# Aggregating a four-head graph-attention layer transposed, in column groups of the array

## The chip, the cores and the metric

One core of a Trainium2 chip runs the whole program. The time is device microseconds from start to end of one execution; the kernel before takes 3029.77 us (median of three runs, 3027.55 to 3030.76). The profile is of one execution with a span of 3030.3 us.

## What is computed

A stack of four graph-attention layers on 32 batch items of 512 nodes with 256 features, all in fp32. Each layer is normalised first and added to its input. Layer 2, which the change touches, has four heads of 64 features:

```python
def _L2_gnn_ref(h, adj, W, a):
    N_H, D_F = (4, 64)
    Wh = (h @ W).reshape(h.shape[0], h.shape[1], N_H, D_F)
    ...
    e = s_src[:, :, None, :] + s_dst[:, None, :, :]
    e = jnp.where(e > 0, e, NEG_SLOPE * e)
    e = jnp.where(mask, e, -jnp.inf)
    alpha = jax.nn.softmax(e, axis=2)
    h_out = jnp.einsum('bijh,bjhd->bihd', alpha, Wh)
    ...
    return jax.nn.elu(h_out)
```

The kernel doesn't form the softmax with an exponential per edge. Since the exponential of a leaky ReLU of a sum is the larger of two products, a common factor of each row can be taken out. What remains for an edge from node j to node i is `p_j * max(r_i, t_j) * mask`. The factor `p_j` is put into the features of node j, so the weights of a head are one maximum and one product per edge, and the sum over j of the same weights with `p_j` alone is the softmax's denominator.

## The kernel before

The 512 nodes are four tiles of 128. Four streams (`NS = 4`) each take every fourth batch item through all the layers. A stream is a generator that yields a due time, worked out in `after_us` from the matmul columns issued so far and a given delay; the main loop always continues the stream that is due first. So the order in which the program is written is a mixture of four batch items in different layers, and each engine executes its part of the order that a scheduler makes of it. TensorE works through one queue for all streams: a matmul that waits holds up those of other streams behind it. Each stream has two banks of PSUM (`bank`, 128 x 512 fp32).

`matmul` (line 66) and `transpose` (line 70) are helpers, so the profile puts all matmuls on L68 and all transposes on L72. A matmul is called with the stationary operand second and the moving operand third: `matmul(p, w, x)` gives `w` transposed times `x`.

Layer 2 (`layer2`, line 424) runs so for each batch item:

- `turned` transposes the normalised input; for each node tile two matmuls with 268 columns (line 430) give, for all four heads, 64 features and three logits (`CH` = 67). ScalarE takes the exponentials of the logits (line 434: `p`, `t`, `r`), and VectorE multiplies the features with `p` (line 435). The tile `v` holds per node and head 64 features times `p`, then `p`, then `t`, `r`.
- `begin(h)` calls `weights` (line 335): four transposes spread `r` of the head along the free axis of a bank, and four VectorE instructions (line 343, 128 x 512 each) make the weights `w` of the head: partition = source node j, free = target node i, one instruction for each tile of j.
- The aggregation of a head (line 457): for each of four tiles of target nodes, four matmuls accumulate over j. The stationary operand is a 128 x 128 block of the weights, the moving operand the 65 columns `v[:, j, h, :D + 1]`: 64 features and `p`. The result has target nodes on partitions, and its 65th column is the denominator.
- One reciprocal (through `reciprocal`, line 359) and one product (line 461) divide; after every second head ScalarE and VectorE form the ELU of both heads and add it to `x` (lines 468 to 470).

The weights of head h + 1 are begun before the aggregation of head h.

Of the kernel before, what the change touches and what calls it, by code (L numbers as in the profile page):

```python
# [19 lines left out]
FP = mybir.dt.float32  # L20
# [3 lines left out]
AF = mybir.ActivationFunctionType  # L24
OP = mybir.AluOpType
# [3 lines left out]
P = 128  # L29
# [7 lines left out]
def fast(ctx, tc, flag, x, adj, w0, a0, w1, a1, w2, a2, mlp1_w, mlp1_b, mlp2_w, mlp2_b,  # L37
         w_fc, a_fc, w_hand, a_hand, out):
    nc = tc.nc
    B, N, F = x.shape  # L40
    NT = N // P
# [3 lines left out]
    NH = a2.shape[0]  # L45
    D = F // NH
# [5 lines left out]
    const = ctx.enter_context(tc.tile_pool(name="const", bufs=1))  # L52
    work = ctx.enter_context(tc.tile_pool(name="work", bufs=2))
# [5 lines left out]
    spent = [0.0]  # L59
    pace = [1.0] * NS  # L60

    def after_us(us):

        return begun[0] + pace[turn[0]] * (STRETCH * spent[0] / CYCLES + SLOW * us)

    def matmul(p, w, x, **flags):
        spent[0] += 4 * max(x.shape[-1], P)
        nc.tensor.matmul(p, w, x, **flags)  # L68

    def transpose(p, x, i):  # L70
        spent[0] += 2 * P
        nc.tensor.transpose(p, x, i)  # L72

    def bank():
        return psum.tile([P, N], FP, tag=f"b{turn[0]}", name="b", bufs=8 // NS)
# [3 lines left out]
    ident = const.tile([P, P], FP, name="ident")  # L79
# [3 lines left out]
    minus1 = const.tile([P, 1], FP, name="minus1")  # L83
    nc.vector.memset(minus1, -1.0)
    seen = const.tile([P, 5 * B], FP, name="seen")

    def load_x(b):
        t = work.tile([P, NT, F], FP, tag="x", name="x", bufs=NS + 1)
        nc.sync.dma_start(t, x[b].rearrange("(t p) f -> p t f", p=P))
        return t  # L90
# [16 lines left out]
    def project(dst, block, k, a_cols):  # L107

        ft, n = a_cols.shape[1], a_cols.shape[2]
        p = bank()  # L110
        for f in range(ft):
            transpose(p[:, f * P:(f + 1) * P], block(k, f), ident)
        wT = work.tile([P, N], FP, tag="y", name="wT", bufs=3)
        nc.scalar.copy(wT[:, :ft * P], p[:, :ft * P])
        q = bank()
        for f in range(ft):
            matmul(
                q[:, :n], wT[:, f * P:(f + 1) * P], a_cols[:, f, :], start=(f == 0), stop=(f == ft - 1)
            )
        nc.vector.tensor_copy(dst, q[:, :n] if len(dst.shape) == 2 else q[:, :n].rearrange("p (h c) -> p h c", c=3))  # L120
# [36 lines left out]
    for h in range(NH):  # L157
        t, r = divmod(h * D, P)
# [38 lines left out]
    for j in range(NT):  # L197
        turn[0] = j % NS
        p = bank()
# [49 lines left out]
    def small(shape, name):  # L249
        return work.tile([P] + shape, FP, tag=name, name=name, bufs=2 * NS)  # L250

    def new_xn():
        return work.tile([P, NT, F], FP, tag="xn", name="xn", bufs=3)

    def norm(xt, xn, rs, t0, late):


        st = small([2, 6], "st")
        mv = small([2, 2], "mv")
        for i in range(2):  # L260
            nc.vector.bn_stats(st[:, i, :], xt[:, t0 + i, :])  # L261
            nc.vector.bn_aggr(mv[:, i, :], st[:, i, :])
        rp = rs[:, t0:t0 + 2]
        nc.scalar.activation(rp, mv[:, :, 1], AF.Ln, bias=eps)
        nc.scalar.activation(rp, rp, AF.Exp, scale=-0.5)
        for i in range(2):
            if late:
                nc.vector.tensor_scalar(
                    xn[:, t0 + i, :], xt[:, t0 + i, :], mv[:, i, 0:1], 0.0, op0=OP.subtract, op1=OP.max
                )  # L270
            else:
                nc.vector.tensor_scalar(  # L272
                    xn[:, t0 + i, :], xt[:, t0 + i, :], mv[:, i, 0:1], rp[:, i:i + 1], op0=OP.subtract, op1=OP.mult
                )
# [9 lines left out]
    def turned(xn, when):  # L284

        hT = work.tile([P, KF, N], FP, tag="hT", name="hT", bufs=3)
        turn_pair(xn, hT, 0)
        yield when
        turn_pair(xn, hT, 2)
        yield after_us(0.6)  # L290
        return hT
# [3 lines left out]
    def note(e):  # L295

        c = next(noted)
        nc.vector.tensor_reduce(seen[:, c:c + 1], e, AX.XY, OP.max)  # L298
# [36 lines left out]
    def weights(r_col, t_col, masked=True):  # L335

        r = bank()
        for t in range(NT):
            transpose(r[:, t * P:(t + 1) * P], r_col(t).to_broadcast([P, P]), ident)
        wt = work.tile([P, NT, N], FP, tag="w", name="w", bufs=4)  # L340
        for j in range(NT):
            if masked:
                nc.vector.scalar_tensor_tensor(  # L343
                    wt[:, j, :], r, t_col(j), maskT[:, j, :], op0=OP.max, op1=OP.mult
                )
            else:
                nc.vector.tensor_scalar(wt[:, j, :], r, t_col(j), None, op0=OP.max)  # L347
        return wt

    def pair(tag="y"):  # L350
        return work.tile([P, 2, F], FP, tag=tag, name=tag, bufs=3)

    def aggregate(p, wt, t, rhs):
        for j in range(NT):
            matmul(p, wt[:, j, t * P:(t + 1) * P], rhs(j), start=(j == 0), stop=(j == NT - 1))

    def reciprocal(den):
        r = small([1], "rden") if len(den.shape) == 2 else small([NH, 1], "rden4")
        nc.vector.reciprocal(r, den)  # L359
        return r  # L360
# [14 lines left out]
    def add_elu(xr, r, q):  # L375

        nc.vector.scalar_tensor_tensor(r, q, 1.0, r, op0=OP.min, op1=OP.add)
        nc.vector.scalar_tensor_tensor(xr, r, -1.0, xr, op0=OP.add, op1=OP.add)
# [45 lines left out]
    def layer2(xt, xn, rs, when):  # L424
        hT = yield from turned(xn, when)
        v = work.tile([P, NT, NH, CH], FP, tag="v", name="v2", bufs=4)
        for t in range(NT):
            ps = bank()
            for k in range(KF):
                matmul(  # L430
                    ps[:, :NH * CH], hT[:, k, t * P:(t + 1) * P], W2[:, k, :, :], start=(k == 0), stop=(k == KF - 1)
                )
            pv = ps[:, :NH * CH].rearrange("p (h c) -> p h c", c=CH)
            nc.scalar.activation(v[:, t, :, D:], pv[:, :, D:], AF.Exp, scale=rs[:, t:t + 1])
            nc.vector.scalar_tensor_tensor(
                v[:, t, :, :D], pv[:, :, :D], rs[:, t:t + 1], v[:, t, :, D:D + 1].to_broadcast([P, NH, D]),
                op0=OP.mult, op1=OP.mult,
            )
            yield after_us(0 if t + 1 < NT else 1)
        ya = work.tile([P, NT, F], FP, tag="y4", name="y4", bufs=2)  # L440
        wts = []

        def begin(h):
            wts.append(weights(lambda t: v[:, t, h, D + 2:D + 3], lambda j: v[:, j, h, D + 1:D + 2]))
            return after_us(3.2)

        when = begin(0)
        note(v.rearrange("p t h c -> p (t h) c")[:, :, D:])
        yield after_us(1)
        for h in range(NH):  # L450
            last = when
            if h + 1 < NH:
                when = begin(h + 1)
            yield last
            wt = wts[h]
            p = bank()
            for t in range(NT):
                aggregate(p[:, t * (D + 1):(t + 1) * (D + 1)], wt, t, lambda j: v[:, j, h, :D + 1])
            pv = p[:, :NT * (D + 1)].rearrange("p (t c) -> p t c", c=D + 1)
            r = reciprocal(pv[:, :, D:])  # L460
            nc.vector.tensor_tensor(
                ya[:, :, h * D:(h + 1) * D], pv[:, :, :D], r.to_broadcast([P, NT, D]), op=OP.mult
            )
            if h % 2:
                c = slice((h - 1) * D, (h + 1) * D)
                y = ya[:, :, c]
                q = pair("q").rearrange("p a (b f) -> p (a b) f", f=2 * D)
                nc.scalar.activation(q, y, AF.Exp)
                nc.scalar.activation(y, y, AF.Relu)
                add_elu(xt[:, :, c], y, q)  # L470
            yield after_us(0)
        xn, rs = new_xn(), small([NT], "rs")
        for t0 in range(0, NT, 2):
            norm(xt, xn, rs, t0, False)
        yield after_us(7)
        return xn, rs, after_us(2)
# [241 lines left out]
    ready = {i: i * LEAD for i in range(NS)}  # L718
# [3 lines left out]
    while ready:  # L722
        i = min(ready, key=ready.get)
# [21 lines left out]
    p = bank()  # L745
# [401 lines left out]
@with_exitstack  # L1147
def kernel(ctx: ExitStack, tc: tile.TileContext, *args):
    nc = tc.nc
    keep = ctx.enter_context(tc.tile_pool(name="keep", bufs=1))  # L1150
    flag = keep.tile([1, 1], I32, name="flag")
    fast(tc, flag, *args)
    bad = nc.values_load(flag[0:1, 0:1], min_val=0, max_val=1)
    with tc.If(bad > 0):
        general(tc, *args)
# [27 lines left out]
```

## Time and profile before

| What | Value | From |
|---|---|---|
| Span of the profiled execution | 3030.3 us | page, first line |
| Mean granted TensorE clock | 0.990 | clocks of the cores |
| Records of TensorE matmuls, all lines | 15529 | page, part 1 |
| Aggregation of layer 2, 65 columns | 4096 records, mean 274 ns | groups with shapes kept apart |
| TensorE waiting for another engine's weights in all layers (weight loads on line 343) | 31.6 us, 73 times | waits |
| First projection to last aggregation of one batch item's layer 2 | 756.4 to 805.2 us | starts of 268- and 65-column records |
| First projection of the next stream's layer 2 | 848.6 us | the same |

The page names engines by short names: PE is TensorE's matmul, PEld its weight load, DVE is VectorE, ACT is ScalarE, POOL is GpSimd. A row of the groups gives the line, the engine, the operation, the tiles written and read, the shape, the count, then the busy time in us and the mean duration in ns of one record, and behind the second bar the idle time of the engine just before these instructions with what ended it. Records of TensorE overlap in the trace, since a matmul's end is modelled with the time it takes to leave the array; so the busy time of a group is the union of its records, and the mean is longer than the distance from one to the next. A row of the timeline merges neighbours of the same line and tiles: start, duration to the end of the last, and how many.

### The profile page before, as it was taken

To read this page: it belongs to the slowest core of one execution; us is meant where nothing else is said; L and a number is where in the kernel's file an instruction comes from. 1 tells how busy PE (TensorE), PEld (TensorE's weight loads), DVE (VectorE), ACT (ScalarE), POOL (GpSimd) and SP (SyncE) were. 2 spreads that over 40 slices of the span, in tenths; PEclk is the share of its full clock that TensorE was granted. 3 is DMA by queue.
4 is the path that set the end of the run, shared out by engine and by line. 5 is a ranking of instruction groups with operands and counts; after the bars stand their busy time and mean duration, and the time that the engine had idled before them with its cause. 6 is when DMAs were issued, how large, how long until landed. Compare 5 with 4: busy or idle time off the path is not lost. (4 is left out here: it accounts for less than half of the span.)

```text
span 3030.3 us, 43501 instructions
## 1 busy us (share of the span) xinstructions
PE 2924.8 (97%) x15529; PEld 2368.3 (78%) x15529; DVE 2269.9 (75%) x5674; ACT 1489.6 (49%) x3758; POOL 470.2 (16%) x509
## 2 busy tenths in 40 slices
PE   7999999999999999999999999999999999999897
PEld 5787887877788877788877788877888877788665
DVE  4588778777877777777778777877877877767664
ACT  3444455554455554455554455554455554454445
POOL 0011111101111201112111111101111111111111
PEclk8999999999999999999999999999999999999999
DMA  3022223222223222223232223222223222212220
GB/s 91 1 88 87 75 74 102 83 90 88 74 74 102 84 89 83 80 74 102 78 95 82 81 74 102 83 90 91 71 74 102 89 84 87 74 52 82 84 97 29
DMA packets 178685, 245.46 MB, mean 81 GB/s; under 512 B 15328, under 2 KB 153886, under 8 KB 178464
## 3 DMA queue, kind: packets, MB, share of 16 engines
q1 hardware_dynamic: 148704, 144.32, 14.9%
q0 software_dynamic: 29760, 98.30, 9.8%
q8 instruction: 125, 2.05, 0.3%
q14 instruction: 96, 0.79, 0.1%
HBM read 127.46 MB, written 115.12 MB: 80 GB/s over the span
## 5 line engine op out<-in xcount | busy, mean ns | idle before, releaser
L68 PE MATMUL b<-v,w 128*128 128x257 f32 (+1 forms) x7232 | 1225.5, 322 | 22.0 <-DVE w L343 8.6
L68 PEld LDWEIGHTS b<-v,w 128*128 128x128 f32 x7232 | 1054.2, 192 | 186.7 <-issue 51.7
L343 DVE SCALAR_TENSOR_TENSOR w<-b,v,maskT 128x512 f32<-128x512 f32 x896 | 635.7, 743 | 13.3 <-PE b L72 10.5
L68 PE MATMUL b<-WFC,oT 128*128 128x256 f32 (+1 forms) x2048 | 491.5, 380 | 0.8 <-ACT v L311 0.5
L68 PEld LDWEIGHTS b<-WFC,oT 128*128 128x128 f32 x2048 | 373.6, 189 | 50.8 <-issue 1.0
L68 PE MATMUL b<-W,hT 128*128 128x259 f32 (+1 forms) x1536 | 389.1, 391 | 9.8 <-DVE v L315 8.6
L68 PEld LDWEIGHTS b<-W,hT 128*128 128x128 f32 x1536 | 282.8, 192 | 60.2 <-DVE v L315 11.0
L571 POOL DMA_INDIRECT order<-v,at x248 | 251.1, 1013 | 462.7 <-DVE seen L298 139.9
L68 PE MATMUL b<-hT,WM 128*128 128x512 f32 x512 | 251.9, 598 | 8.2 <-ACT hT L282 7.8
L359 DVE RECIPROCAL rden<-b 128x1 f32<-128x1 f32 (+1 forms) x516 | 80.2, 163 | 233.6 <-PE b L68 230.6
L677 POOL TENSOR_TENSOR x<-x,y 128x512 f32<-128x512 f32 x64 | 81.2, 1269 | 1077.3 <-ACT y L675 980.8
L619 POOL DMA_INDIRECT g<-table,at x124 | 122.5, 988 | 790.8 <-ACT y L639 287.1
L68 PE MATMUL b<-oT,WM 128*128 128x512 f32 x512 | 232.8, 597 | 0.0
L261 DVE BATCH_NORM_STATS2 st<-x 128x6 f32<-128x256 f32 x512 | 193.2, 409 | 5.6 <-DMA x<-in_x_dram 2.7
L331 ACT ACTIVATE oT<-b,bias 128x512 f32<-128x512 f32 x128 | 87.5, 686 | 216.6 <-PE b L68 216.4
L384 DVE TENSOR_TENSOR y<-q,y 128x512 f32<-128x512 f32 x192 | 132.5, 691 | 67.1 <-ACT q L383 48.2
L72 PEld LDWEIGHTS b<-ident,xn 128*128 128x128 f32 x1024 | 125.9, 142 | 69.9 <-DVE xn L272 23.6
L493 ACT ACTIVATE v<-b,ends 128x256 f32<-128x256 f32 x256 | 120.3, 470 | 122.2 <-PE b L68 115.6
L72 PE MATMUL b<-ident,xn 128*128 128x128 f32 x1024 | 159.7, 278 | 20.4 <-DVE xn L272 8.7
L282 ACT ACTIVATE hT<-b 128x512 f32<-128x512 f32 x256 | 150.2, 593 | 40.7 <-PE b L72 39.6
L68 PEld LDWEIGHTS b<-oT,WM 128*128 128x128 f32 x512 | 95.3, 191 | 93.5 <-issue 91.4
L638 ACT ACTIVATE q<-g,rden 128x512 f32<-128x512 f32 x124 | 89.5, 722 | 145.9 <-DVE rden L359 142.7
(139 smaller groups left out, 3735.0 us busy)
## 6 DMA issues: line engine op xcount, KB each, us to landing
table<-sums SPq DMA_DIRECT2D x62, 1032.0 KB
sums<-order SPq DMA_DIRECT2D x62, 516.0 KB
x<-in_x_dram SPq DMA_DIRECT2D x32, 512.0 KB
out_dram<-x SPq DMA_DIRECT2D x64, 256.0 KB
sums<-order SPq DMA_DIRECT2D x62, 129.0 KB
order<-v,at POOLq DMA_INDIRECT x248, 2.5
g<-table,at POOLq DMA_INDIRECT x124, 4.5
adj<-in_adj_dram SPq DMA_DIRECT2D x1, 1024.0 KB
```

Source lines behind the costliest of these rows:

```text
L68: nc.tensor.matmul(p, w, x, **flags)
L72: nc.tensor.transpose(p, x, i)
L261: nc.vector.bn_stats(st[:, i, :], xt[:, t0 + i, :])
L282: nc.scalar.activation(hT[:, :, t0 * P:(t0 + 2) * P], p.rearrange("p (k n) -> p k n", k=KF), AF.Relu)
L331: nc.scalar.activation(o[:, f, :], p, AF.Relu, bias=bias[:, f:f + 1])
L343: nc.vector.scalar_tensor_tensor(wt[:, j, :], r, t_col(j), maskT[:, j, :], op0=OP.max, op1=OP.mult)
L384: nc.vector.tensor_tensor(r, q, r, op=OP.add)
L493: nc.scalar.activation(halves[c][:, t, :F], ps[:, :F], AF.Copy, scale=ends[:, t, 0:1])
L571: nc.gpsimd.indirect_dma_start(out=orders[c], out_offset=bass.IndirectOffsetOnAxis(ap=at[:, 0, t:t + 1], axis=0), in_=halves[c][:, t, :], ...
L619: nc.gpsimd.indirect_dma_start(out=g, out_offset=None, in_=table, in_offset=bass.IndirectOffsetOnAxis(ap=at[:, 1, t:t + 1], axis=0),)
L638: nc.scalar.activation(q, z, AF.Exp, scale=rd)
L677: nc.gpsimd.tensor_tensor(xr, xr, y, op=OP.add)
```

## The change

The aggregation of layer 2 is turned round. The features become the stationary operand (64 columns) and the weights the moving one (512 columns), so that the result has features on partitions and target nodes along the free axis. Two heads are done together: head `a` writes partitions 0 to 63 of a bank and head `a + 1` partitions 64 to 127, which puts their matmuls in two column groups of 64 columns of TensorE's array. Eight matmuls (four tiles of j, two heads) replace 32.

The denominators are no longer a 65th column. A tile `sums_of_p` holds for each node, tile and head 32 columns, of which the first is `p` and the others zero. For each pair of heads 16 matmuls with these 32 columns as stationary operand and 256 target nodes as moving operand use four column groups of 32: two heads times two halves of the target nodes.

Both results are copied to SBUF by ScalarE (`aT`, `dT`) and transposed back in six transposes per pair, after which the division and the ELU go on as before. Both runs of matmuls are in a block of high priority so that nothing of another stream comes between them, and the order over j and heads in the first is reversed so that its first matmul is the one whose weights come last. `begin` for the two heads of the next pair is now called between the runs of the present one. The helper `matmul` charges a half or a quarter of the columns in the planner's account (`beside`) for these matmuls. The output tile `y4` holds two heads instead of four and has one buffer instead of two.

```diff
-    def matmul(p, w, x, **flags):
-        spent[0] += 4 * max(x.shape[-1], P)
-        nc.tensor.matmul(p, w, x, **flags)
+    def matmul(p, w, x, beside=1, **flags):
+        spent[0] += 4 * max(x.shape[-1], P) / beside
+        return nc.tensor.matmul(p, w, x, **flags)
...
+    sums_of_p = const.tile([P, NT, NH, 32], FP, name="sums_of_p")
+    nc.vector.memset(sums_of_p, 0.0)
...
             nc.scalar.activation(v[:, t, :, D:], pv[:, :, D:], AF.Exp, scale=rs[:, t:t + 1])
+            nc.scalar.activation(sums_of_p[:, t, :, 0:1], pv[:, :, D:D + 1], AF.Exp, scale=rs[:, t:t + 1])
...
-        ya = work.tile([P, NT, F], FP, tag="y4", name="y4", bufs=2)
...
-        when = begin(0)
+        begin(0)
         note(v.rearrange("p t h c -> p (t h) c")[:, :, D:])
         yield after_us(1)
-        for h in range(NH):
-            last = when
-            if h + 1 < NH:
-                when = begin(h + 1)
-            yield last
-            wt = wts[h]
+        begin(1)
+        ready = after_us(6)
+        for a in range(0, NH, 2):
+            yield ready
+            aT = work.tile([P, N], FP, tag="aT", name="aT", bufs=1)
             p = bank()
-            for t in range(NT):
-                aggregate(p[:, t * (D + 1):(t + 1) * (D + 1)], wt, t, lambda j: v[:, j, h, :D + 1])
-            pv = p[:, :NT * (D + 1)].rearrange("p (t c) -> p t c", c=D + 1)
-            r = reciprocal(pv[:, :, D:])
-            nc.vector.tensor_tensor(
-                ya[:, :, h * D:(h + 1) * D], pv[:, :, :D], r.to_broadcast([P, NT, D]), op=OP.mult
-            )
...
+            with tc.high_priority():
+                for j in range(NT)[::-1]:
+                    for h in (1, 0):
+                        matmul(
+                            p[h * D:(h + 1) * D, :], v[:, j, a + h, :D], wts[a + h][:, j, :], beside=2,
+                            start=(j == NT - 1), stop=(j == 0),
+                        )
+            nc.scalar.copy(aT, p)
             yield after_us(0)
+            dT = work.tile([P, HN], FP, tag="dT", name="dT", bufs=1)
+            p = bank()
+            with tc.high_priority():
+                for j in range(NT):
+                    for i in range(2):
+                        for h in range(2):
+                            g = 32 * (2 * i + h)
+                            m = matmul(
+                                p[g:g + 32, :HN], sums_of_p[:, j, a + h, :], wts[a + h][:, j, i * HN:(i + 1) * HN],
+                                beside=4, start=(j == 0), stop=(j == NT - 1),
+                            )
+                            if j + g == 0:
+                                tc.keep_in_program_order(m)
+            nc.scalar.copy(dT, p[:, :HN])
+            when = after_us(0.8)
+            y = work.tile([P, NT, 2 * D], FP, tag="y4", name="y4", bufs=1)
+            for i in range(2):
+                if a + 2 < NH:
+                    yield after_us(0)
+                    begin(a + 2 + i)
+                    ready = after_us(5)
+                yield when
+                p = bank()
+                for c, part in enumerate((aT[:, i * P:], aT[:, (2 + i) * P:], dT[:, i * P:])):
+                    transpose(p[:, c * P:(c + 1) * P], part[:, :P], ident)
+                r = small([2, 2, 1], "rden4")
+                nc.vector.reciprocal(r, p[:, 2 * P:3 * P].rearrange("p (i h c) -> p i h c", i=2, h=2)[:, :, :, 0:1])
...
```

More of the change, by code (lines that the diff above doesn't have):

```diff
@@ L439, in layer2 @@
             yield after_us(0 if t + 1 < NT else 1)
-        ya = work.tile([P, NT, F], FP, tag="y4", name="y4", bufs=2)
+        HN = N // 2
         wts = []
@@ L444, in begin @@
             wts.append(weights(lambda t: v[:, t, h, D + 2:D + 3], lambda j: v[:, j, h, D + 1:D + 2]))
-            return after_us(3.2)
-        when = begin(0)
+        begin(0)
         note(v.rearrange("p t h c -> p (t h) c")[:, :, D:])
         yield after_us(1)
-        for h in range(NH):
-            last = when
-            if h + 1 < NH:
-                when = begin(h + 1)
-            yield last
-            wt = wts[h]
-            p = bank()
-            for t in range(NT):
-                aggregate(p[:, t * (D + 1):(t + 1) * (D + 1)], wt, t, lambda j: v[:, j, h, :D + 1])
-            pv = p[:, :NT * (D + 1)].rearrange("p (t c) -> p t c", c=D + 1)
-            r = reciprocal(pv[:, :, D:])
-            nc.vector.tensor_tensor(
-                ya[:, :, h * D:(h + 1) * D], pv[:, :, :D], r.to_broadcast([P, NT, D]), op=OP.mult
-            )
[L464 to L470, printed above, removed]
-            yield after_us(0)
@@ new lines, in layer2 @@
+        begin(1)
[3 more added lines that the diff above has]
+            aT = work.tile([P, N], FP, tag="aT", name="aT", bufs=1)
+            p = bank()
+            with tc.high_priority():
[6 more added lines that the diff above has]
+            nc.scalar.copy(aT, p)
+            yield after_us(0)
+            dT = work.tile([P, HN], FP, tag="dT", name="dT", bufs=1)
[25 more added lines that the diff above has]
+                nc.vector.reciprocal(r, p[:, 2 * P:3 * P].rearrange("p (i h c) -> p i h c", i=2, h=2)[:, :, :, 0:1])
+                nc.vector.tensor_tensor(
+                    y.rearrange("p (k i) (h d) -> p k i h d", k=2, h=2)[:, :, i, :, :],
+                    p[:, :2 * P].rearrange("p (k h d) -> p k h d", k=2, h=2), r.to_broadcast([P, 2, 2, D]), op=OP.mult
+                )
+                when = after_us(0)
+            c = slice(a * D, (a + 2) * D)
+            q = pair("q").rearrange("p a (b f) -> p (a b) f", f=2 * D)
+            nc.scalar.activation(q, y, AF.Exp)
+            nc.scalar.activation(y, y, AF.Relu)
+            add_elu(xt[:, :, c], y, q)
@@ L472, in layer2 @@
+        yield after_us(0)
         xn, rs = new_xn(), small([NT], "rs")
```

## Prediction

> **What bounds the kernel now.** I read the page's first two parts first: which engine is full, and whether it is full all the time.
>
> ```profile
> PE 2924.8 (97%) x15529; PEld 2368.3 (78%) x15529; DVE 2269.9 (75%) x5674; ACT 1489.6 (49%) x3758; POOL 470.2 (16%) x509
> ...
> PE   7999999999999999999999999999999999999897
> ...
> PEclk8999999999999999999999999999999999999999
> ```
>
> TensorE is busy 97% of the span in every slice but the ends, at full clock. VectorE follows at 75%. So a change is worth what it adds to or takes from TensorE's stream, as long as it makes TensorE wait no longer. Next, the groups of instructions with shapes kept apart, for what layer 2 puts into that stream:
>
> ```profile
> L68 PE MATMUL b<-v,w 128*128 128x65 f32 x4096 | 476.9, 274 | 5.7 <-DVE y L461 2.0 <-DVE seen L298 1.2 <-DVE at L566 1.2
> L68 PE MATMUL b<-WFC,oT 128*128 128x256 f32 x1024 | 245.9, 380 | 0.8 <-ACT v L311 0.5 <-ACT tj L545 0.3
> L68 PE MATMUL b<-oT,WM 128*128 128x512 f32 x512 | 232.8, 597 | 0.0
> L72 PE MATMUL b<-ident,v 128*128 128x128 f32 x896 | 132.5, 274 | 11.8 <-DVE v L315 11.8
> L343 DVE SCALAR_TENSOR_TENSOR w<-b,v,maskT 128x512 f32<-128x512 f32 x896 | 635.7, 743 | 13.3 <-PE b L72 10.5
> ```
>
> The program issues 32 batches x 4 heads x 16 = 2048 matmuls with 65 columns, and the trace has 4096 records: one fp32 matmul is two records. A transpose is one (896 = 224 x 4). The means (274 ns) contain a tail that overlaps the next record, so the price is the pitch, read from stretches of one shape in the timeline:
>
> ```profile
> 1499.74 0.83 PE L68 MATMUL b<-v,w 128*128 128x65 f32 x6
> 1500.41 2.81 PE L68 MATMUL b<-WFC,oT 128*128 128x256 f32 x12
> ...
> 1503.49 1.03 PE L68 MATMUL b<-WFC,oT 128*128 128x256 f32 x4
> 1504.35 0.60 PE L72 MATMUL b<-ident,v 128*128 128x128 f32 x4
> 1504.79 0.60 PE L68 MATMUL b<-v,w 128*128 128x257 f32 x2
> ...
> 1516.75 3.65 PE L68 MATMUL b<-oT,WM 128*128 128x512 f32 x8
> 1520.24 1.00 PE L68 MATMUL b<-v,w 128*128 128x65 f32 x8
> ```
>
> From the start of one row to the start of the next: six 65-column records take 0.67 us, **112 ns** each; four of 256 take 0.86 us, **215**; eight of 512 take 3.49 us, **436**; four transposes 0.44 us, **110**. A 65-column record costs half of a 256-column one for a quarter of the columns: that waste is what the change goes after. 4096 x 112 ns = 459 us, 15% of the span.
>
> **What the Trainium skill says.** (1) "TensorE: Matmul & The Clock Gate", section LDWEIGHTS: a weight load takes its columns divided by 1.2 GHz, whatever the moving operand. For 128 columns that is 107 ns; the 112 ns of a 65-column record agree. (2) "FP8 and Floating Point Precision", TensorE Precision Notes: true fp32 is four passes through the array. The trace shows two records per matmul, each some twice its columns long (215 ns for 256): four passes in two records, both of one instruction and so of one column group. (3) "TensorEngine Tiling (Array Packing)", Key Properties: tiles of the array run in parallel, and a change of tiling mode drains the engine. No matmul of the kernel before is tiled, so the trace is silent. (4) "TensorE: Matmul & The Clock Gate", Part 3, The mechanism: matmuls start and end in program order; only weight loads are pulled ahead. No record of before contradicts it, and none tests it with groups.
>
> **The change part by part** (per pair of heads; there are 32 x 2 = 64 pairs).
>
> Removed: 32 matmuls of 65 columns, 64 records x 112 ns = 7.17 us.
>
> Added, features: 8 matmuls with 64 stationary columns and 512 moving ones, 16 records of 436 ns. Heads alternate between two column groups. By (2) the two records of one matmul share a group, so they follow each other; by (4) the next matmul, in the other group, can't start before the second record of this one has. What overlaps is then the second record of one matmul with the first of the next: 8 matmuls take 9 slots, 9 x 436 = 3.92 us. Bounds: 8 x 436 = 3.49 if the groups are fully free of each other, 16 x 436 = 6.98 if groups don't overlap in fp32.
>
> Added, sums of p: 16 matmuls with 32 stationary columns and 256 moving ones in four groups, 32 records of 215 ns. **Here is the choice that decides.** If four groups ran freely, 8 x 215 = 1.72 us. By the same argument as above only neighbours overlap, two at a time, however many groups there are: 17 x 215 = 3.66 us. In series it would be 6.88. I take 3.66.
>
> Added, transposes: 6 x 110 ns = 0.66 us, in whole-array mode.
>
> Added, changes of mode: into and out of each of the two tiled runs, up to four per pair. A drain is bounded below by 0 and above by the tail of a record, 380 - 215 = 165 ns (256-column row). Half: 4 x 0.083 = 0.33 us. In the issue order of the changed kernel all 64 feature runs stand as 8 in a row and all 64 runs of sums as 16 in a row, so there are no more changes than that.
>
> Sum on TensorE: 3.92 + 3.66 + 0.66 + 0.33 = 8.57 against 7.17: +1.40 us a pair, x 64 = **+90 us**.
>
> Waits: a feature run starts only when the weights of both heads are there, 8 x 743 ns = 5.9 us of VectorE, and stands at the head of TensorE's queue with the other streams' matmuls behind it. In the new order some 6 to 9 us of TensorE work lie between the first head's transposes and its run, so the slack is 0 to 3 us where VectorE is prompt. Before, TensorE's weight loads waited for these weights 31.6 us in all. I take +5 us net, between -20 and +40.
>
> ScalarE: per batch four more small exponentials (172 to 272 ns, rows of lines 311 and 434) and copies of 512 and 256 columns (578 and 371 ns, rows of lines 545 and 604), two of each: about 2.8 us, x 32 = 90 us on an engine that is busy 1490 of 3030. At nothing: three other streams' matmuls stand between the copies and the transposes that need them. VectorE keeps four reciprocals and four 256-element products per batch (176 and 416 ns): nothing. The single buffers of sums_of_p, aT, dT and y4 are shared by the streams, but layer 2 of a batch lasts some 48 us (first projection 756.4, last aggregation 805.2), and the next stream's begins 92 us after it (848.6): nothing. The zeroing of sums_of_p lies in the load of the first data: nothing.
>
> **The rivals.**
> - *Two at a time* (forecast): 3029.8 + 90 + 5 = 3125, of which I take 3120, since some sum runs follow their feature run at once, which saves a change of mode. For it: two records per matmul, program order. It needs nothing beyond what the trace and the skill say.
> - *Groups run free*: 3.49 + 1.72 + 0.66 + 0.33 = 6.20 us, -0.97 a pair, -62 us, +5 of waits: about 2973. This is what the change counts on (it charges a half and a quarter for such matmuls), and the Part 3 of (4) reports 2.38 times for three column groups. Against it: no statement there has two records per matmul. With full drains and late weights it shrinks to 2995.
> - *No overlap in fp32*: 6.98 + 6.88 + 0.66 + 0.2 = 14.7 us, +7.5 a pair, +480 us: about 3510. The reported speed-up speaks against it.
> - *The weights arrive late*: with groups free but 1 us of waiting at each of 64 feature runs, -62 + 64: 3030, no change. VectorE at 75% speaks for some of it, the 31.6 us of before against so much.
>
> **How the numbers follow.** Two at a time 0.48, groups free 0.38, no overlap 0.07, late weights with free groups 0.07. The predicted time is that of the first. Its own spread, with 0 to 165 ns per drain and -20 to +40 us of waits, is 3090 to 3165; that of free groups 2945 to 3000. The range 2960 to 3155 holds both but their ends, and leaves out about 2 in 10 (no overlap, the deepest gain, the worst loss). Faster: 0.37 of free groups, 0.03 of late weights, 0.03 for a cause I haven't seen: 0.43. Same 0.04. Slower 0.53.
>
> **What would show it.** In the timeline of the changed kernel: 16 feature records in 3.5 to 4 us (first start to next group's start) show the two-fold overlap, 7 us its absence. The 32 records of sums settle the rest: about 3.7 us two at a time, 1.7 us groups free. A gap of over 0.1 us at the change between 64-, 32- and 128-column runs would be the drain. Waits of weight loads for the weights' line well above 31.6 us would show late weights. The prediction is wrong if the sums' 16 matmuls take under 2.5 us, or if TensorE's busy share falls.

## The result and the profile after

The changed kernel takes 3190.59 us (median of four runs, 3186.94 to 3203.52) against 3030.27 us for the kernel before: 5.4% longer (ratio 1.0538, interval 1.0507 to 1.0570), 160 us. The direction was forecast, the size was not, and the time lies above the range. What the trace shows is not what was forecast either.

First the page of the changed kernel:

```profile
span 3191.3 us, 42500 instructions
PE 2946.3 (92%) x14889; PEld 2085.8 (65%) x14889; DVE 2285.5 (72%) x5675; ACT 1592.4 (50%) x4014; POOL 474.2 (15%) x509
```

TensorE's busy share fell from 97% to 92%, and so did VectorE's, from 75% to 72%. No engine has become the bound. TensorE has 640 records fewer and stands idle more: 245.0 us outside its busy time against 105.5 before.

The two tiled runs in the timeline of the changed kernel (start, duration to the end of the last record, number of records):

```profile
1468.02 0.60 PE L69 MATMUL b<-W,hT 128*128 128x259 f32 x2
1468.55 3.65 PE L69 MATMUL b<-w,v 128*64 128x512 f32 x16
1472.14 0.70 PE L69 MATMUL b<-W,hT 128*128 128x259 f32 x2
...
1480.53 1.46 PE L69 MATMUL b<-WFC,oT 128*128 128x256 f32 x6
1481.91 1.93 PE L69 MATMUL b<-w,sums_of_p 128*32 128x256 f32 x32
1483.78 0.66 PE L73 MATMUL b<-ident,y 128*128 128x128 f32 x4
```

From start to start the 16 feature records take 3.59 us and the 32 records of sums 1.87 us. Eight records of 512 columns one behind the other are 8 x 0.43 = 3.44 us, eight of 256 columns 8 x 0.215 = 1.72 us. So each column group works through its own eight records and the groups don't hold each other up: two-fold overlap for the features, four-fold for the sums. The rest, 0.15 us in each run, is the change of mode at its end (0.09 us) and a slower start (the second record of a group comes 0.48 instead of 0.43 us behind the first in the features, 0.24 instead of 0.215 in the sums); the change into the mode is the excess of the rows ahead (1480.53 to 1481.91 is 1.38 us for six records of 215 ns: 0.09 us). Per pair of heads: 3.59 + 1.87 + 0.18 + 0.66 for six transposes = 6.30 us, against 7.17 before. **The array's part of the change is a gain**, 0.87 us a pair, 56 us in all.

So 160 + 56 = some 216 us were lost elsewhere. 140 of them are the added idle time. A second part is the clock that TensorE was granted, of which the page's row of digits shows little, since a 9 stands for 90% or more: its mean fell from 0.990 to 0.975. The clock records of the traces have two values only, full and half, and the time at half rose from 57.7 to 157.8 us. This is one such place in the changed kernel:

```profile
2274.57 0.33 PE L73 MATMUL b<-ident,dT 128*128 128x128 f32 x1 [2.37 <-ACT dT L484]
...
2277.02 1.94 PE L69 MATMUL b<-WHA,rT 128*128 128x259 f32 x4
2278.74 1.23 PE L69 MATMUL b<-W,hT 128*128 128x259 f32 x4
2279.81 1.04 PE L69 MATMUL b<-WHA,rT 128*128 128x259 f32 x4
2280.69 1.04 PE L69 MATMUL b<-W,hT 128*128 128x259 f32 x4
```

The bracket is a wait of 2.37 us for the copy of the sums. From 2275.7 to 2279.1 us the granted clock was a half. In that stretch four records of 259 columns take 1.72 us from start to start; four of the same kind take 0.88 us right behind it. In all, TensorE was busy at half clock for 123.2 us against 47.1 before; since records take twice as long there, half of the difference, 38 us, is time lost. Some 38 us of the 216 remain: they lie inside TensorE's busy time at full clock and were not traced further. The half clock comes behind waits: in all 20 traces kept here, from 60 us on, each of the 496 stretches at half clock begins when TensorE has stood idle for at least 0.7 of the 3.4 us before. That the waits bring it about is read from this order in time; no run tests it.

Who made TensorE's matmuls wait, in the changed kernel (total us, times, longest):

```profile
PE b L73 <- DVE y L388: 45.6, 27, 6.5
PE b L73 <- ACT dT L484: 17.6, 6, 4.4
PE b L69 <- ACT hT L286: 17.6, 18, 1.8
PE b L73 <- DVE xn L276: 17.2, 24, 3.1
PE b L69 <- DVE w L347: 16.3, 13, 5.2
PE b L73 <- DVE xn L272: 14.9, 10, 4.5
```

and the same lines in the kernel before (each line number is now four higher: L272 is now L276, L343 L347, L268 L272, L384 L388):

```profile
PE b L72 <- DVE xn L272: 8.7, 22, 2.0
PE b L68 <- DVE w L343: 8.6, 14, 1.2
...
PE b L72 <- DVE xn L268: 5.4, 5, 1.7
PE b L72 <- DVE y L384: 4.1, 4, 2.3
```

Two things stand out. The waits are spread over all layers: line 388 belongs to layer 3, lines 272 and 276 to the norms between layers, line 286 to the turned input. Of these lines only `dT` and 10.5 us of `w` are layer 2's own; further down the list follow 18.4 us for `rden` of line 497, its division. And single waits are long, up to 6.5 us, where in these lines of before the longest was 2.3. The work on lines 388, 272, 276 and 286 is the same as before. So what differs should be where it stands in the queues of the other engines when TensorE arrives; the experiments test this.

### The profile page after: what moved, and what is told of

It is laid out like the page before. It is cut to its first block, busy times and chain, and to the rows that moved or that the text cites. A ratio compares the mean times of both kernels' runs of the same rounds, so it can differ in the third digit from the quotient of the medians.

```text
span 3191.3 us, 42500 instructions
## 1 busy us (share of the span) xinstructions
PE 2946.3 (92%) x14889; PEld 2085.8 (65%) x14889; DVE 2285.5 (72%) x5675; ACT 1592.4 (50%) x4014; POOL 474.2 (15%) x509
## 4 chain that ended last, share of the span: by engine, by line
PE 57%; DVE 25%; DMA 7%; ACT 6%; issue 3%; SPq 1%; POOL 0%; POOLq 0%; ACTq 0%; DVEq 0%
PE b L69 51%; PE b L73 7%; DVE w L347 5%; DMA sums<-order 3%; DVE st L265 3%; DMA order<-v,at 2%; DVE xn L276 1%; DVE sums L645 1%; DVE junk L587 1%; DVE y L388 1%; DVE y L381 1%; DVE x L382 1%; DVE sums L642 1%; DVE sums L633 1%; DVE g L671 1%
## 5 line engine op out<-in xcount | busy, mean ns | idle before, releaser
L69 PE MATMUL b<-v,w 128*128 128x257 f32 x3136 | 773.8, 388 | 18.1 <-ACT y L416 7.9
L69 PEld LDWEIGHTS b<-v,w 128*128 128x128 f32 x3136 | 579.6, 192 | 176.0 <-issue 28.5
L347 DVE SCALAR_TENSOR_TENSOR w<-b,v,maskT 128x512 f32<-128x512 f32 x896 | 621.7, 742 | 46.0 <-PE b L73 44.5
L69 PE MATMUL b<-W,hT 128*128 128x259 f32 (+1 forms) x1536 | 400.1, 393 | 14.3 <-DVE v L319 10.4
L69 PE MATMUL b<-w,v 128*64 128x512 f32 x1024 | 242.2, 616 | 23.1 <-DVE rden L497 12.6
L73 PE MATMUL b<-ident,xn 128*128 128x128 f32 x1024 | 172.8, 287 | 43.4 <-DVE xn L276 17.2
L388 DVE TENSOR_TENSOR y<-q,y 128x512 f32<-128x512 f32 x192 | 132.4, 690 | 72.3 <-ACT q L387 50.6
L69 PEld LDWEIGHTS b<-w,v 128*64 128x64 f32 x1024 | 72.0, 140 | 160.1 <-issue 150.1
L268 ACT ACTIVATE rs<-mv,eps 128x2 f32<-128x2 f32 x256 | 74.6, 292 | 187.3 <-DVE mv L266 183.3
L363 DVE RECIPROCAL rden<-b 128x1 f32<-128x1 f32 x388 | 58.8, 159 | 140.8 <-PE b L69 136.4
```

Of the source, the lines that this page charges most:

```text
L69: return nc.tensor.matmul(p, w, x, **flags)
L347: nc.vector.scalar_tensor_tensor(wt[:, j, :], r, t_col(j), maskT[:, j, :], op0=OP.max, op1=OP.mult)
L388: nc.vector.tensor_tensor(r, q, r, op=OP.add)
```

## The experiments

All are compared with the kernel before on the same chip. The expectations name these theories of the 216 us. L: layer 2 lost the overlap between one head's aggregation and the next head's weights. P: the blocks of high priority push other streams aside. C: the planner charges tiled matmuls too little. S: the four streams are no longer evenly spaced. R: the plan of due times for layer 2 is longer, which gives the other layers less of the other streams' work between their steps. Q: matmuls stand in TensorE's queue before their inputs exist. F: the issue order fits or doesn't, by accident of the constants. "Plan" is the sum of the due times of one batch item, added up from the source in the planner's own unit: 297.2 before, 315.3 after.

**Staging alone, in the kernel before** (the edit is shortened).

```diff
-        for h in range(NH):            # begin(h + 1), then aggregate h
+        begin(1); ready = after_us(6)
+        for a in range(0, NH, 2):      # aggregate a and a + 1, then begin(a + 2), begin(a + 3)
```

> The kernel before with the change's staging alone: the weights of both heads of a pair begun together, both heads then aggregated with the old 65-column matmuls, and the weights of the next pair begun only after that. No tiled matmul, no copy, no transpose back. Theory L (the chain of layer 2 got longer because the weights of the next heads are no longer made beside the aggregation; the streams go round more slowly): well over half of the loss comes back here, 3100 to 3190 us, and the time from the first projection of layer 2 to the next layer's first matmul grows from 58 us towards 75. Theory P (the runs of high priority push the other streams' work aside): within 0.5% of before, 3015 to 3045. Theory C (the planner's half and quarter charges shift the streams): the same, 3015 to 3045.

Measured 3158.32 us, ratio 1.0431 (1.0412 to 1.0449), with the old 65-column matmuls. From the first projection of layer 2 to layer 3's first matmul it takes 81 us (58 before, 79 after). So a loss of 128 us, four fifths of the change's, comes without a tiled matmul, a copy or a block of high priority. P and C are not needed for one of that size. The edit brings new due times with it, though (its plan is 318.6), so it doesn't tell the staging from the plan.

**No pause between features and sums.**

```diff
             nc.scalar.copy(aT, p)
-            yield after_us(0)
             dT = work.tile(...)
```

> The changed kernel with one pause taken away: the sums of p are issued right behind the features of the same pair, where the changed kernel first gives the other streams a turn (in its trace the first sum stands 12 to 19 us behind the first feature). Theory L: layer 2 of a batch item gets 15 to 25 us shorter, and the time falls to 3060 to 3130. Theory P: two runs of high priority in a row hold the others up for longer, so no better, 3180 to 3230. Theory C: 3180 to 3200.

3236.14 us, 1.0681 (1.0658 to 1.0705): slower, and layer 2 did not get shorter (82 us). L expected the opposite.

**One head at a time** (the edit is shortened).

```diff
-    matmul(p[h * D:(h + 1) * D, :], v[:, j, a + h, :D], wts[a + h][:, j, :], ...)
+    matmul(p[i * D:(i + 1) * D, :HN], v[:, j, h, :D], wt[:, j, i * HN:(i + 1) * HN], ...)
...
+    when = begin(h + 1)               # ahead of the runs of head h
```

> The changed kernel with one head at a time: the two 64-column groups take the two halves of one head's target nodes (256 columns each) and the four 32-column groups the quarters of them (128 each), both into one bank, one copy of 384 columns and three transposes per head; the weights of head h+1 are begun before head h is aggregated, as in the kernel before. The array's work is that of the changed kernel but for one or two more changes of mode per pair (92 ns each). Theory L: the gain on the array comes through, 2940 to 3010. Theory P: twice as many runs of high priority, 3190 or more. Theory C: the charges are as in the changed kernel, 3150 to 3200.

3114.37 us, 1.0282 (1.0261 to 1.0303). Better than the change, far from a gain, although its plan is 297.5 and layer 2 takes 60 us, both close to before. If the part that came back is L's, it is at most half of the loss; later runs differ by more for constants of the plan alone.

**Full charge in the planner.**

```diff
-        spent[0] += 4 * max(x.shape[-1], P) / beside
+        spent[0] += 4 * max(x.shape[-1], P)
```

> The changed kernel with the planner's charge for tiled matmuls put back to the full columns (no half, no quarter), so the due times in layer 2 lie later; nothing else. Theory C: back to 3000 to 3080. Theory L: layer 2 gets longer still by its own account, 3190 to 3260. Theory P: no difference, 3180 to 3200.

3411.28 us, 1.1244 (1.1213 to 1.1275). C is wrong in its direction, and L's number too low by far. One line that touches no instruction moved the time by 221 us (the plan is now 349.4): the planner's due times became the suspect.

**The streams evenly spaced.**

```diff
-    LEAD = 75.0
+    LEAD = 78.8
```

> The changed kernel with one constant of the planner changed: LEAD, the distance in due time at which the four streams start, 78.8 instead of 75. The due times of one batch item, added up from the source, come to 297.2 in the kernel before (four times 74.3, so a LEAD of 75 spaces the streams evenly) and to 315.3 in the changed one (75, 75, 75 and 90.3). Theory S (the streams run unevenly spaced since the plan of layer 2 got longer, and meet in the same stages): half of the loss or more comes back, 3050 to 3115. Theory L (the lost overlap inside layer 2): spacing matters little, 3165 to 3195.

3125.52 us, 1.0317 (1.0299 to 1.0334): 65 us back, 40% of the loss, by a constant. In the steady part of the trace the batch items now follow each other at 93.0 us, one like the other.

**The kernel before with a longer plan,** once with LEAD as it was, once even.

```diff
-            yield after_us(0 if t + 1 < NT else 1)
+            yield after_us(0 if t + 1 < NT else 13)
```

> The kernel before with 18 due-time units of delay in layer 2 (behind the last projection), so that its plan is as long as the changed kernel's (315.2) with LEAD 75 as it was; all instructions are those of before. Theory S: 3080 to 3150. Theory L: a later start of the weights alone breaks no overlap, 3025 to 3060.

> The same as e6_before_delay, with LEAD 78.8, so the plan is as long but the streams are even. Theory S: back to 3025 to 3050. If it is the length of layer 2 in the plan and not the spacing, as slow as e6_before_delay, over 3080. Theory L: 3025 to 3060.

3132.78 us, 1.0339 (1.0322 to 1.0357), and with LEAD 78.8 3253.55 us, 1.0727 (1.0706 to 1.0748). These are the instructions of the kernel before, all of them: constants of the plan alone cost 102 and 223 us. Even spacing, which helped the changed kernel, harms here: S falls. L can't explain e6 and e7 either, since the weights still overlap the aggregation.

**One head at a time, due later.**

```diff
-    LEAD = 75.0
+    LEAD = 77.4
...
-            return after_us(3.2)
+            return after_us(5.5)
...
-            yield after_us(0.8)
+            yield after_us(2.5)
```

> e3_headwise with later due times: the tiled runs due 5.5 instead of 3.2 after their weights are begun, the transposes 2.5 instead of 0.8 after the runs, and LEAD 77.4 for its plan of 309.5. In the trace of e3_headwise TensorE stood idle for 50.5 us before the runs of features and for 34 us before the transposes of their copies. If these waits at the head of TensorE's queue are what is left of the loss (theory Q: matmuls are put into the queue before their inputs exist), 3000 to 3060. If it is the length of the chain through copy and transposes (theory L), a later due time makes it longer: 3110 to 3150.

3286.98 us, 1.0847 (1.0829 to 1.0866). The wait before the feature runs fell from 50.5 to 11.6 us as Q expected (of the 50.5, 41.1 were for the division of a head before, line 485, and 1.4 for the weights), that of the transposes from 21.8 us (the expectations of this run and of e11 put it at 34) to 1.2, and the time rose by 173 us. In this run's trace the waits appear elsewhere:

```profile
PE b L73 <- ACT rs L268: 82.0, 28, 6.4
PE b L69 <- DVE sums L621: 72.9, 27, 4.8
```

The first is the norm between layers, the second the sort in layer 3. A wait taken from one place of TensorE's queue came back in others. The mean granted clock was 0.957 here and 0.985 in e3_headwise.

**The changed kernel with the old length of plan.**

```diff
-        ready = after_us(6)
+        ready = after_us(1)
...
-                    ready = after_us(5)
+                    ready = after_us(0)
```

> The changed kernel with its plan of layer 2 shortened to about that of the kernel before: the waits for the weights 1 and 0 instead of 6 and 5, which brings the due times of one batch item from 315.3 to 300.3; LEAD 75 as it is. Theory R (the loss is the longer plan of layer 2: the issue order gives this layer more and all other layers less of the other streams' work to lie between their steps): most of the loss comes back, 2980 to 3060. Theory Q (matmuls are put into TensorE's queue before their inputs exist): the tiled runs now wait for their weights, 3180 to 3260.

3028.77 us over 12 runs, ratio 0.9997 (0.9988 to 1.0006). **The whole loss is gone**, with every instruction of the change in place and two numbers of the plan changed. R expected this, Q the opposite. Its page:

```profile
span 3024.6 us, 42547 instructions
PE 2894.3 (96%) x14889; PEld 2072.0 (69%) x14889; DVE 2263.4 (75%) x5675; ACT 1572.8 (52%) x4014; POOL 466.9 (15%) x509
```

and of its waits, the line that was the first of the changed kernel's:

```profile
PE b L73 <- DVE y L388: 5.4, 5, 1.6
```

TensorE is back at 96%, and the line that waited 45.6 us waits 5.4. In the steady part a batch item comes every 89.3 us (357.3 us for four) against 90.7 before (362.8), so some of the array's gain arrives there; the first four items reach layer 2 within 256 us of each other's first against 235 before, which takes half of it away again.

**A longer plan elsewhere.**

```diff
-        sort = after_us(11)
+        sort = after_us(23)
```

> The kernel before with the same 18 due-time units of delay as e6_before_delay, but in layer 3, where a stream waits for the sorted rows anyway; plan 315.2, LEAD 75. Theory R (any longer plan takes from the others): as slow as e6_before_delay, 3100 to 3160. If only a delay in layer 2 costs: 3025 to 3050.

3188.88 us, 1.0530 (1.0508 to 1.0551), again with the instructions of the kernel before. A delay makes a loss in either place, though not the same one: 158 us here, 102 in e6_before_delay.

**One head at a time, transposes a step later.**

```diff
             yield last
+            if h:
+                finish(h - 1, pT)     # transposes, division
             wt = wts[h]
```

> e3_headwise with the transposes and the division of head h moved in front of the tiled runs of head h+1, so that their copy has a whole step to arrive, and with no added pause: plan 296.9 with LEAD 75, as before. Theory R together with Q: the 34 us of waits before the transposes go, and with them some more: 3040 to 3090. If the gain on the array came through: below 3030.

3190.74 us, 1.0527 (1.0509 to 1.0545), with a plan of 296.9. R fails here: the length of the plan is as before and the time is not.

**No priority.**

```diff
-            with tc.high_priority():
+            if True:
...
-                            if j + g == 0:
-                                tc.keep_in_program_order(m)
```

> The changed kernel without the blocks of high priority and without the pin on the first matmul of the sums, so that the scheduler may put other matmuls between the tiled ones: more changes of mode at 92 ns each. Theory P (the priority is what disturbs the other streams): 3060 to 3130. Theories R and Q: the breaks cost something, 3190 to 3260.

3203.96 us, 1.0574 (1.0552 to 1.0595). The runs did break (106 and 81 unbroken pieces of features and sums instead of 64 of each), and nothing was gained: P falls.

**Each of the two pauses alone, and none.** These are the lines as they stand in each run; the changed kernel has 6, 5, 0.8 and 75.

```diff
 e13:  ready = after_us(1)   ready = after_us(5)
 e14:  ready = after_us(6)   ready = after_us(0)
 e15:  ready = after_us(0)   ready = after_us(0)   when = after_us(0)   LEAD = 74.0
```

> The changed kernel with the first of the two pauses alone shortened (the weights of the first pair: 1 instead of 6); plan 307.8, LEAD 75. Theory R (the length of the plan, wherever it comes from): half way between 3029 and 3190, 3080 to 3140, and the same as e14_second_pause. If one pause does it all, this one is near 3030 or near 3190.

> The changed kernel with the second of the two pauses alone shortened (the weights of the second pair: 0 instead of 5); plan 307.8, LEAD 75. Theory R: the same as e13_first_pause, 3080 to 3140. Otherwise near 3030 or near 3190.

> The changed kernel with no pause left in layer 2 (0, 0 and 0 instead of 6, 5 and 0.8), plan 296.4, LEAD 74 to fit it. Theory R: faster than e9_short_plan, 2985 to 3025. Theory Q (matmuls queued before their inputs exist): slower, 3040 to 3150, with waits before the tiled runs.

3159.61 us (1.0429, 1.0409 to 1.0450), 3350.46 us (1.1053, 1.1034 to 1.1071) and 3287.23 us (1.0837, 1.0819 to 1.0855). Two kernels with the same length of plan (307.8) are 191 us apart, and the shortest plan of all (296.4, even) is slow. R is finished as a rule.

**A single constant beside the good one.**

```diff
-    LEAD = 75.0
+    LEAD = 74.0
```

> e9_short_plan with LEAD 74 instead of 75 (plan 300.3, so the streams start closer and the fourth distance is 78.3). In e9_short_plan the first four batch items reach layer 2 over 256 us against 235 before, which ate half of the gain of its steady part. If the start is what is missing: 3010 to 3027. If even spacing matters more: 3030 to 3080.

3231.01 us, 1.0656 (1.0636 to 1.0676): 202 us more than e9_short_plan. Here a part of the cause can be read in the timeline, at several places such as this one:

```profile
193.60 1.07 PE L69 MATMUL b<-w,v 128*64 128x512 f32 x2
194.61 0.62 PE L69 MATMUL b<-w,sums_of_p 128*32 128x256 f32 x2
195.16 1.07 PE L69 MATMUL b<-w,v 128*64 128x512 f32 x2
196.16 0.62 PE L69 MATMUL b<-w,sums_of_p 128*32 128x256 f32 x2
```

Two records are one matmul. The two kinds of tiled matmul alternate, one by one. A feature matmul alone takes 1.01 us from start to start instead of 3.59 / 8 = 0.45, one of the sums 0.55 instead of 1.87 / 16 = 0.12: no neighbour in another group to overlap with, and a change of mode for each. Sums and features stand side by side in this issue order, and both are of high priority. There are 192 unbroken pieces of features here, 78 in e9_short_plan and 64 in the changed kernel. Distances from each tiled record to the next record, waits among them included, add up to 502 us here and 370 us in e9_short_plan: 133 of the 207 us between the two spans. The same happened in e14 (195 pieces) and e15 (236).

**The same constant in the kernel before.**

```diff
-    LEAD = 75.0
+    LEAD = 74.0        # and, in the second, 76.0
```

> The kernel before with LEAD 74 instead of 75 (its plan is 297.2, so the streams become almost even: 74, 74, 74 and 75.2). No instruction differs. Theory R (time goes by length and evenness of the plan): 3015 to 3035. Theory F (the issue order fits or doesn't, by accident, and the kernel before sits at a place that was found for it): 3070 to 3250. If the jumps come from the tiled runs alone: 3020 to 3040.

> The kernel before with LEAD 76 (76, 76, 76 and 69.2). No instruction differs. Theory R: a little slower, 3035 to 3070. Theory F: 3070 to 3250. If the jumps come from the tiled runs alone: 3030 to 3050.

LEAD 74: 3054.60 us, 1.0079 (1.0060 to 1.0099). LEAD 76: 3109.38 us, 1.0264 (1.0237 to 1.0292). The kernel before sits at the best of the three values, and a step of one unit costs 22 us on one side, 77 on the other. F holds for it too, though with a smaller step than theory F gave for LEAD 74. Broken runs, which it can't have, are part of the jumps in e14, e15 and e16; they don't explain e4 (71 pieces), nor e7, which moved the kernel before by 223 us.

**What the waits and the clock took.** The traces of the runs above show this as well. Idle is the span without TensorE's busy time.

| Kernel | Span, us | TensorE idle, us | TensorE busy at half clock, us |
|---|---|---|---|
| before | 3030.3 | 105.5 | 47.1 |
| e9_short_plan | 3024.6 | 130.4 | 53.9 |
| e5_even_lead | 3121.4 | 180.3 | 54.5 |
| changed | 3191.3 | 245.0 | 123.2 |
| e10_before_delay_sort | 3189.0 | 186.6 | 186.5 |
| e7_before_delay_even | 3262.1 | 193.1 | 258.8 |
| e4_full_charge | 3415.5 | 370.5 | 259.2 |

In e7_before_delay_even, with the instructions of the kernel before, TensorE is idle for 88 us more and loses half of 212 us to the clock: 194 of the 232 us between the spans. In e10_before_delay_sort it is 81 and 70 of 159. So a wait costs more than its own length, and two issue orders with about as many waits can differ in the clock: e5 and e7 do.

## Why the prediction was wrong

- **What bounds the kernel**: right, and e9_short_plan runs at 96% again. But the full clock was read from digits that don't tell 90% from 100%, and no term of the sum stood for a change of the clock.
- **Features, "8 matmuls take 9 slots"**: 3.92 us predicted, 3.59 measured with the change of mode at the end, so 8 slots. The 436 ns of a slot came from one stretch; most records of 512 columns stand 429 ns apart.
- **Sums, "here is the choice that decides"**: this step failed. It took two at a time, 3.66 us; the trace has 1.87, four at a time, which is the term of the rival *groups run free*. The argument was that the two records of one fp32 matmul share a group and that matmuls start in program order, as "TensorE: Matmul & The Clock Gate", Part 3, The mechanism, says. In the trace the first records of the four groups start within 20 ns of each other, and the second ones 0.24 us later, side by side again. A matmul of the sums that stands alone in e16_short_lead74 has its two records the same 0.24 us apart. So a second record that waits for its group does not hold up the next matmul. The matmuls themselves still start in order; the measurement decides against what was concluded from the sentence, that the next one can't start before the second record of this one.
- **Changes of mode**: 0.33 us a pair predicted (half of the bound), about 0.48 measured with the slower start of a run. That a change of tiling mode drains the engine, as "TensorEngine Tiling (Array Packing)", Key Properties, says, agrees with the trace: 0.09 us each way.
- **The sum on TensorE**: +90 us predicted, -56 measured. The rival said -62.
- **Waits, "+5 us net, between -20 and +40"**: some +216, of which 140 are idle time, 38 the half clock, and 38 not traced. This is the other failed step and the one that decides the result. It looked at the one wait that the change adds by design, for the weights. That one indeed grew little (8.6 to 16.3 us of matmuls waiting for `w`; weight loads waited for it 32.7 us, against 31.6). What it left out is that the change rewrites the due times of layer 2, and that all other streams' matmuls are put in order by due times; e9_short_plan, e6_before_delay and e10_before_delay_sort show that these numbers alone make or undo a loss of this size.
- **ScalarE "at nothing"**: not quite; the transposes waited 17.6 us for the copy of the sums, in six places.
- **Single buffers "nothing"**: no run contradicts it: e9_short_plan has the same single buffers and no loss, and e11_headwise_pipe, with two of `aT`, is as slow as the change.
- The prediction named two signs of being wrong, sums under 2.5 us and a falling busy share of TensorE; both came true. That the direction was right nevertheless was luck: two errors of opposite sign were made, one too dear (the array, by 146 us) and one too cheap (the waits, by 211). The rival *late weights* had the right kind of cause, waiting that eats the gain of free groups, but with under a third of the size and for the wrong instruction.

What stays open: why a given set of constants fits and its neighbour doesn't. Length of plan, even spacing and priority were each tried and none orders the 19 times. Shown is that the loss sits in the issue order and not in the instructions: e9_short_plan has those of the change without the loss, e6, e7 and e10 have those of before with one. How an order costs time is shown in good part: waits of TensorE, the half clock behind them, and in e14, e15 and e16 broken tiled runs. Which waits a chosen order will give was not predictable from the plan. No version here beats the kernel before clearly; e9_short_plan equals it.

## What to carry to other kernels

In a kernel whose streams are interleaved by a hand-tuned plan, a change has two effects: what it does to the instructions, and that it moves the plan off the place where it was tuned. Measure the second by itself, with a kernel that has the old instructions and the new due times, and tune the constants anew before the change is judged. Look at the mean granted clock to three digits beside the idle time: here a wait of a microsecond or two was often followed by several at half clock. Putting small fp32 matmuls into column groups took 0.87 of 7.17 us a pair off TensorE's stream, as long as the groups' matmuls stood in one unbroken run. Where two tilings alternated, priority did not keep them apart; an order that does was not tried.

## What the runs showed of the hardware

- fp32 matmuls in different column groups overlap fully, across both records of a matmul: 32 records of 256 columns in four groups took 1.87 us with the change of mode out, where one group's eight come to 1.72 at the pitch of the untiled ones (0.215 us).
- A tiled matmul with no neighbour in another group costs 1.01 us (512 columns) and 0.55 us (256 columns), both records and the change of mode included, against 0.45 and 0.12 in an unbroken run (e16_short_lead74).
- A change of tiling mode costs 0.09 us on the way in and 0.09 us on the way out; with the slower start of a run the way out comes to 0.15 us.
- The granted clock in these traces is full or half. At half clock the records of the changed kernel stand twice as far apart: 853 against 429 ns with 512 columns, 213 against 109 for a transpose. Stretches at half clock last 3.4 us or multiples of it, and each of the 496 in the 20 traces follows at least 0.7 us of idle time within the 3.4 us before.
